# A graph network with experts on one Trainium2 core: edge stages in a fixed program order with work in small pieces, and VectorE's two-tensor operations reading both operands from SBUF

## The chip, the cores and the metric

The kernel runs on one core of a Trainium2 chip. The metric is the device time of one launch, in microseconds (us); lower is better. The time before is 2635.79 us, the median of three runs (2631.52 to 2639.92).

## The reference, cut to what matters

`x` has 3,125 nodes of 256 numbers. There are 53,125 edges (each node's edge to itself among them), each with a source, a destination, one of 200 types and a weight, all in float32 or int32. Four blocks follow one another, and each adds its result to `x`:

```python
ln = layernorm                                   # over the 256 numbers, no scale or offset
# 1: attention over neighbours, 4 heads of 64
feats = ln(x) @ Ws + bs                          # 4 heads
w = exp(-relu((a_s[src] + a_d[dst] + aw_e * edge_weight + ab) / 20))
x = x + segment_sum(w * feats[dst], src) / segment_sum(w, src)
# 2: 16 experts, each node through its best two
x = x + sum over top 2 of p_e * ((silu(ln(x) @ w1_e) * (ln(x) @ w2_e)) @ w3_e)
# 3: relations; h = ln(x)
W = W3 @ a                                       # three parts: source, destination, type
alpha = exp(leaky_relu(h[src] @ W_s + h[dst] @ W_d + rel[type] @ W_r))
alpha = alpha / sum(alpha, axis=1)               # over an axis of one element
agg = segment_sum((h[src] + rel[type]) @ weight_neighbor * alpha, dst)
x = x + relu(agg) + h @ (loop_weight where the node has an edge, else evolve_loop_weight)
# 4: FFN (256 to 1024 to 256, gelu) of the best half of the nodes by a score; h = ln(x)
s = h @ wr + br
x = x + (h + (gelu(h @ w1 + b1) @ w2 + b2) * s where the rank of s < 1561, else h)
```

## The kernel before, in words

**Tiles.** Nodes lie in 25 tiles of 128, one node per partition. Edges are sorted by the node that receives, so each node tile has its own stretch of edge tiles of 128 edges: 18 for a full tile, 8 for the last, 440 in all. Edge tiles are taken in groups of up to six (`GRP`), never across a node tile: 74 groups (`edge_groups`, L714).

**Stages in order** (`run`, L1477). Sort of the edges for the first layer (`sort_edges`, L310: a ranking that is a generator, whose `yield`s mark where other work may go between; then 13 moves, L545 to L569; then `load`, L578). Layer norm and features of the first layer, written to DRAM as `table0` (`heads_features`, L828). First edge stage, E0 (`heads_edges`, L881). Top two of 16 experts and the experts on 65 tiles of rows (`experts`, L989), and at the end of it 50 gathers `yg` (L1170) that fetch each node's two results, weighted and added to `x` by VectorE (L1174). Features of the second layer: products of its weights with `w3a` (L1203), tables of the types, layer norm `xn2`, and `table1` in DRAM (`relations_features`, L1181, with the store at L1270). Second edge stage, E1 (`relations_edges`, L1272, with `load` of the second sort ahead of it). Ranking of the nodes and FFN (`depths`, L1367).

**An edge stage** has three stages per group, which are functions that `edge_stages` (L724) returns. `gather`: for the first group of a node tile, SP fetches the node numbers of all its edges into every partition (`spread`, L739); GpSimd issues six indirect DMAs, one per edge tile, that bring one table row per edge into `rows` (L754, three buffers); VectorE makes `oh`, the one-hot of the receiving node per edge (L762, 128 x 768 numbers), and `hot` (L771), which has nodes or types on the partitions. `message`: TensorE multiplies `hot` with the receiving nodes' part of the score (L780), VectorE reduces it (L787), adds the parts of the score, and ScalarE takes exp. In E0 VectorE then multiplies the rows with the weights into `msg` (L926). In E1 it writes the one-hot of the type behind the row in `rows` (L1313, 200 numbers), and ScalarE scales `oh` into `ohw` (L1319). `add`: TensorE multiplies `oh` and `msg`, or `ohw` and `rows`, into the sums of the node tile (L798), and after its last group VectorE adds what lies beyond (`acc`) and calls `finish`. In E0 that divides by the sum of weights, adds to `x` and calls `done` of `gate` (L949), which for each five node tiles does the layer norm, stores it as `xtab` for the experts and computes the logits. In E1 it is L1324: loop weights and relations.

**What sets the order.** `pipelined` (L811) emits, for each step, one piece of the fill (in E0 the ranking of the second sort), then `gather` of group g, `message` of g-1 and `add` of g-2. This is the order in which the program is traced, not the order of issue: a list scheduler of the framework then orders each engine's instructions by its own estimates of when they are ready. [...]

**Operands in PSUM.** `edge_stages` takes a bank of PSUM, `hold`. It keeps `numbers` (0, 1, 2, ... along the free axis, a copy of an `iota`), which `oh` and the one-hot of the type compare with, and `weights_ps`, into which ScalarE writes the exp a second time for `msg` to read. So `oh`, `msg` and the type's one-hot each read one operand from PSUM and one from SBUF. One pool of PSUM serves the whole kernel: two tiles of 1024 numbers (`A`) and four of 512 (`B`).

**Ranking.** `depths` normalizes all nodes (`xn3`), takes the scores `wc`, turns them into a row `wrow` on every partition and, for each tile, counts the nodes that stand ahead of each of its nodes: `cmp` (L1426), over all 3,125, and `eq` (L1431) for ties. Only then does the FFN begin (L1445 on), four node tiles at a time.

Of the kernel before, what the change touches and what calls it, by code (L numbers as in the profile page):

```python
# [18 lines left out]
P = 128  # L19
# [3 lines left out]
class _Kernel:  # L23
# [12 lines left out]
    def __init__(self, ctx, tc, a, out):  # L36
# [18 lines left out]
        for b in range(self.NT):  # L55
# [7 lines left out]
        assert self.MT % self.KB == 0  # L63
# [3 lines left out]
        self.psum = ctx.enter_context(  # L67
            tc.tile_pool(name="psum", bufs=1, space=bass.MemoryType.PSUM)
        )
# [5 lines left out]

    def ps_a(self, name):
        return self.psum.tile([P, 1024], F32, tag="A", name=name, bufs=2)

    def ps_b(self, name):
        return self.psum.tile([P, 512], F32, tag="B", name=name, bufs=4)  # L80
# [17 lines left out]
    def constants(self):  # L98
# [14 lines left out]
        iota_i = self.work.tile([P, 512], I32, name="iota_i", bufs=1)  # L113
        nc.gpsimd.iota(iota_i, pattern=[[1, 512]], base=0, channel_multiplier=0)
        self.iota = c.tile([P, 512], F32, name="iota")
        nc.vector.tensor_copy(self.iota, iota_i)
# [51 lines left out]
    def transposed(self, src, n, name, evac=None):  # L168

        nc, c = self.nc, n // P  # L170
        pt = self.ps_b(f"ps_{name}")
        for i in range(c):
            nc.tensor.transpose(pt[:, i * P : (i + 1) * P], src[:, i * P : (i + 1) * P], self.ident)  # L173
        dst = self.work.tile([P, c, P], F32, tag=f"T{c}", name=name, bufs=3)
        (evac or nc.scalar.copy)(dst.rearrange("p c q -> p (c q)"), pt[:, :n])  # L175
        return dst
# [133 lines left out]
    def sort_edges(self, pool, rp, name, seg, other, value, bits, tab, help, roomy):  # L310
# [23 lines left out]
        def load_in():  # L334
# [6 lines left out]
            yield  # L341
# [23 lines left out]
            yield  # L365

        def places():
# [4 lines left out]
            for b0 in range(0, NT, piece):  # L372
                m = min(piece, NT - b0)
                hot = tl([P, piece, EC], BF16, "hot", bufs=1)
                for b in range(b0, b0 + m):
                    eng = nc.vector if b % 3 == 0 else help
                    eng.tensor_scalar(hot[:, b - b0, :], bf, float(b), None, op0=OP.is_equal)
                    if b % 6 == 5:
                        yield
                hv = hot.rearrange("p b (s t) -> p b s t", t=C)  # L380
                for w, ps in ((self.ones_h, tot), (self.before_h, pre)):
# [5 lines left out]
                    yield  # L387
# [39 lines left out]
            yield  # L427
# [3 lines left out]
            for b in range(NT):  # L431
# [13 lines left out]
                yield  # L445
# [39 lines left out]
            for s in range(NS):  # L485
# [13 lines left out]
                if s % 3 == 2:  # L499
                    yield  # L500
# [77 lines left out]
        def load():  # L578
# [4 lines left out]
            wide = [self.dram.tile([MT, P], BF16, name=f"{name}_w{i}") for i in range(1 + (not bits))]  # L583
            with tc.tile_pool(name=f"{name}_back", bufs=1) as bp:
# [13 lines left out]
                def turned(v):  # L598
                    pt = self.psum.tile([P, 1024], F16, tag="B", name=f"{name}_pt", bufs=4)
# [13 lines left out]
                for i, w in enumerate(wide):  # L613
                    wb = bp.tile([P, nb, P], BF16, name=f"{name}_wb{i}")
                    nc.vector.tensor_copy(wb[:m], tk[:m, :, :, 1 + i])
                    nc.sync.dma_start(w.rearrange("(i k) p -> k i p", k=m), wb[:m])
# [107 lines left out]
    def edge_stages(self, pool, st, table, width, into, near, others, messages, W, sums, finish):  # L724
# [4 lines left out]
        nc, G = self.nc, self.GRP  # L729
        nv = near.shape[3]  # L730
        now = {}


        hold, sums2 = self.ps_a("ps_hold"), self.ps_a("ps_sums")
        numbers = hold[:, :256]
        nc.vector.tensor_copy(numbers, self.iota[:, :256])
        self.numbers, self.weights_ps = numbers, hold[:, 512:]

        def spread(i, b):  # L739

            t = pool.tile([P, self.tiles[0] // 2, 2 * P + 8], BF16, name=f"wide{i}")
            src = st["wide"][i][self.first[b] : self.first[b] + self.tiles[b], :]
            src = src.rearrange("(o k i) p -> o k (i p)", o=1, i=2)
            nc.sync.dma_start(
                t[:, : self.tiles[b] // 2, : 2 * P], src.to_broadcast([P, self.tiles[b] // 2, 2 * P])
            )
            return t

        def gather(g, b, k, n, head, last):
            if head:  # L750
                now[b] = [spread(i, b) for i in range(len(st["wide"]))]
            rows = pool.tile([P, G, into], F32, name="rows", bufs=3)
            for j in range(n):
# [5 lines left out]
                )  # L759
            sh = [P, n, P]  # L760
            oh = pool.tile([P, G, P], F32, name="oh", bufs=3)
# [4 lines left out]
            lo = (k - self.first[b]) // 2  # L766
            hots = []
            for i, (at, _) in enumerate([(self.pcol1, None)] + others):
                w = now[b][min(i, 1)][:, lo : lo + n // 2, : 2 * P]
                t = pool.tile([P, G // 2, 2 * P], BF16, name=f"hot{i}", bufs=2)  # L770
                nc.vector.tensor_scalar(t[:, : n // 2, :], w, at, None, op0=OP.is_equal)  # L771
                hots.append(t)
            return rows, oh, hots

        def message(g, b, k, n, head, last, rows, oh, hots):
            pe = self.ps_b("ps_near")
            picks = [near[:, b]] + [v for _, v in others]
            for j in range(n):
                for i, (t, v) in enumerate(zip(hots, picks)):
# [6 lines left out]
            own = pool.tile([P, G, nv], F32, name="near")  # L786
# [4 lines left out]
            return messages(k, n, rows, own, oh)  # L791

        def add(g, b, k, n, head, last, oh, msg):
            if head:
                now["sum"] = sums2[:, b % 2 * 512 : (b % 2 + 1) * 512]
            ps = now["sum"]
            for j in range(n):
                nc.tensor.matmul(  # L798
                    ps[:, :W], oh[:, j, :], msg[:, j, :],
                    start=(head and j == 0), stop=(last and j == n - 1),  # L800
                )
            if last:
                more = pool.tile([P, W], F32, name="more")
                nc.sync.dma_start(more, sums[b])
                acc = pool.tile([P, W], F32, name="acc")
                nc.vector.tensor_add(acc, ps[:, :W], more)
                finish(b, acc)

        return gather, message, add

    def pipelined(self, stages, fill=()):  # L811


        groups, done = self.edge_groups(), {}
        fill = iter(fill)
        for step in range(len(groups) + len(stages) - 1):
            if step > 2:
                next(fill, None)
            for i, stage in enumerate(stages):
                g = step - i  # L820
                if 0 <= g < len(groups):
                    done[g] = stage(g, *groups[g], *(done.pop(g, None) or ()))
        for _ in fill:
            pass
# [56 lines left out]
    def heads_edges(self, st, fill, done):  # L881
# [26 lines left out]
        with self.tc.tile_pool(name="edge0", bufs=2) as pool:  # L908
# [7 lines left out]
            def messages(k, n, rows, near, oh):  # L916
# [6 lines left out]
                w = self.weights_ps[:, : n * H].rearrange("p (j h) -> p j h", h=H)  # L923
                nc.scalar.activation(w, s, AF.Exp)  # L924
                nc.scalar.activation(msg[:, :n, HO:], s, AF.Exp)
# [7 lines left out]
            def finish(b, acc):  # L933
# [7 lines left out]
                done(b)  # L941

            self.pipelined(self.edge_stages(
                pool, st, self.table0, W, W, near, [], messages, W, self.sums0, finish
            ), fill)
# [3 lines left out]
    def gate(self, pool):  # L949
# [16 lines left out]
        def done(b):  # L966
# [4 lines left out]
            self.norm_tiles(xn, t0, t1)  # L971
            nc.sync.dma_start(xv[:, t0:t1, :], xn[:, t0:t1, :])
            pl = self.ps_b("ps_logit")
            for t in range(t0, t1):
                xt = self.transposed(xn[:, t, :], D, "x_t")
                for c in range(C):
                    nc.tensor.matmul(
                        pl[:, (t - t0) * NE : (t - t0 + 1) * NE], xt[:, c, :], gw[:, c, :],
                        start=(c == 0), stop=(c == C - 1),
                    )  # L980
            nc.vector.tensor_tensor(
                self.logits[:, t0:t1, :],
# [575 lines left out]
```

## Time and profile before

| | us |
|---|---|
| median of three runs | 2635.79 |
| profiled execution, its own time | 2845.15 |
| its span in the trace | 2842.8 |
| TensorE busy / weight loads | 1878.6 / 1126.4 |
| VectorE busy | 1446.3 |
| ScalarE busy | 390.7 |
| GpSimd busy | 1167.4 |
| mean granted TensorE clock | 0.822 of full |

The profiled execution is 209 us longer than the median; durations below are from it. By operations in the timeline, the stages are: sort and first features up to 430 us, E0 to 1178, routing to 1217, experts to 1718, gather of the results to 1791, second features to 1870, E1 to 2563, ranking to 2682, FFN to the end.

How to read it: a row of operations gives line, engine, operation, output and inputs, number, then busy time and mean duration in ns, then the engine's idle time just ahead of them and what ended it ("issue" is time in which nothing that the profile shows was awaited). Engines are PE (TensorE), PEld (its weight loads), DVE (VectorE), ACT (ScalarE), POOL (GpSimd) and SP (which issues DMAs). In the table by stretch each engine has its busy time and its number of instructions, followed by the granted clock, the share of time that DMA engines were busy, and GB/s. The timeline has start, duration, engine, line and operation.

### The profile page before, as it was taken

The numbers are of one execution on the slowest core, as the hardware profiler recorded it, in microseconds if no ns is written. First come the engines' busy times: TensorE is split into PE (matmuls) and PEld (weight loads), VectorE is DVE, ScalarE is ACT, GpSimd is POOL, SyncE is SP. The second block draws the span as 40 slices with busy tenths as digits, with TensorE's granted clock in tenths as the row PEclk, the third lists the DMA queues.
The fourth block names the chain that finished last, engine by engine and source line by source line (L and its number), as shares of the span: only waits on it lengthen the run. The fifth ranks groups of instructions, "written<-read, shape, count | busy, mean of one in ns | idle before, by whom it ended". The sixth has DMA issues, their size and how long they took to land.

```text
span 2842.8 us, 24381 instructions
## 1 busy us (share of the span) xinstructions
PE 1878.6 (66%) x7534; PEld 1126.4 (40%) x7534; DVE 1446.3 (51%) x3397; ACT 390.7 (14%) x1097; POOL 1167.4 (41%) x1198
## 2 busy tenths in 40 slices
PE   3169554854544443399999991447878778785298
PEld 0024232543433332356666660323434334343166
DVE  4876225476665343644422224445655556549721
ACT  0000010010000000100112120112222222221012
POOL 4235306576654646034411115036666666650000
PEclk9999996676666667577799996768889888898599
DMA  2000325343444433144499982254545455431000
GB/s 83 0 3 5 104 89 137 93 130 112 115 100 114 116 100 101 49 150 130 131 316 318 317 291 84 87 156 131 148 129 148 130 142 149 128 85 34 8 21 18
DMA packets 258938, 334.04 MB, mean 118 GB/s; under 512 B 30861, under 2 KB 192407, under 8 KB 258807
## 3 DMA queue, kind: packets, MB, share of 16 engines
q1 hardware_dynamic: 197527, 191.26, 21.3%
q0 software_dynamic: 51920, 132.68, 17.6%
q10 hardware_dynamic: 9360, 8.52, 0.9%
q8 instruction: 61, 1.00, 0.1%
q14 instruction: 70, 0.57, 0.1%
HBM read 298.38 MB, written 33.98 MB: 117 GB/s over the span
## 4 chain that ended last, share of the span: by engine, by line
PE 39%; DVE 14%; issue 10%; POOL 9%; another core or an unknown queue 8%; DMA 4%; ACT 1%; SPq 0%; DVEq 0%; POOLq 0%; ACTq 0%
PE ps_sums L798 10%; PE ps_h L1130 9%; POOL rows L754 9%; PE ps_y L1147 4%; PE s_mv L560 3%; DVE cmp L1426 3%; PE ps_hid L1453 3%; PE ps_out L1464 3%; DMA rows<-table,s_idx 3%; DVE msg L926 2%; DVE hot L771 2%; PE ps_x_t L173 1%; PE ps_h_t L173 1%; PE ps_f L1264 1%
## 5 line engine op out<-in xcount | busy, mean ns | idle before, releaser
L754 POOL DMA_INDIRECT rows<-table,s_idx x880 | 848.6, 964 | 725.0 <-issue 240.4
L798 PE MATMUL ps_sums<-msg,oh 128*128 128x260 f32 x880 | 306.6, 519 | 261.8 <-DVE msg L926 143.1
L798 PE MATMUL ps_sums<-rows,ohw 128*128 128x457 f32 x880 | 414.0, 616 | 62.8 <-ACT ohw L1319 54.1
L798 PEld LDWEIGHTS ps_sums<-msg,oh 128*128 128x128 f32 x880 | 226.6, 265 | 325.1 <-issue 250.1
L560 PE MATMUL s_mv<-s_hv,s_hp 128*128 128x200 f16 (+1 forms) x832 | 246.8, 472 | 89.9 <-DVE s_hv L555 89.9
L798 PEld LDWEIGHTS ps_sums<-rows,ohw 128*128 128x128 f32 x880 | 179.0, 215 | 217.5 <-issue 149.6
L1130 PE MATMUL ps_h<-w,x_t 128*128 128x512 f32 x520 | 256.1, 638 | 0.0
L771 DVE TENSOR_SCALAR hot<-wide,pcols 128x768 bf16<-128x768 bf16 (+1 forms) x296 | 175.4, 597 | 73.9 <-PE ps_near L780 63.0
L560 PEld LDWEIGHTS <-s_hp 128*128 128x128 f16 x832 | 122.1, 147 | 208.7 <-issue 180.3
L762 DVE TENSOR_TENSOR oh<-ps_hold,s_row 128x768 f32<-128x768 f32 (+1 forms) x148 | 139.9, 946 | 125.7 <-remote 73.5
L1119 POOL DMA_INDIRECT xg<-xtab,who x65 | 61.9, 952 | 345.1 <-PE ps_x_t L173 302.6
L569 POOL DMA_INDIRECT s_tab<-s_rec,s_to x130 | 147.8, 1137 | 115.1 <-ACT s_rec L566 78.9
L780 PEld LDWEIGHTS <-hot 128*128 128x128 bf16 x1760 | 70.0, 98 | 212.3 <-issue 149.2
L1136 DVE TENSOR_TENSOR hid<-hid,ps_h 128x512 f32<-128x512 f32 x65 | 44.7, 688 | 210.3 <-ACT hid L1135 204.4
L1319 ACT ACTIVATE ohw<-oh,s 128x128 f32<-128x128 f32 x440 | 136.5, 388 | 106.6 <-DVE s L1282 75.2
L1130 PEld LDWEIGHTS ps_h<-w,x_t 128*128 128x128 f32 x520 | 102.8, 209 | 105.7 <-issue 105.5
L926 DVE TENSOR_TENSOR msg<-rows,ps_hold 128x1536 f32<-128x1536 f32 x74 | 128.1, 1731 | 2.0 <-ACT ps_hold L924 1.9
L787 DVE TENSOR_REDUCE near<-ps_near 128x24 f32<-128x72 f32 (+2 forms) x148 | 29.4, 198 | 190.3 <-remote 150.2
L1147 PE MATMUL ps_y<-w,h_t 128*128 128x256 f32 x520 | 122.9, 379 | 0.7 <-ACT h_t L175 0.7
L1147 PEld LDWEIGHTS ps_y<-w,h_t 128*128 128x128 f32 x520 | 98.7, 190 | 41.7 <-issue 30.6
L545 DVE TENSOR_TENSOR s_hp<-num_p,s_pp 128x1024 f16<-128x1024 f16 x104 | 71.8, 690 | 82.8 <-PE s_mv L560 81.4
L1313 DVE TENSOR_TENSOR rows<-ps_hold,s_val 128x1200 f32<-128x1200 f32 x74 | 101.1, 1367 | 6.1 <-PE ps_sums L798 6.1
(307 smaller groups left out, 2344.2 us busy)
## 6 DMA issues: line engine op xcount, KB each, us to landing
w<-in_L_ffn_w_dram SPq DMA_DIRECT2D x195, 512.0 KB
wide<-s_w SPq DMA_DIRECT2D x72, 576.0 KB
rows<-table,s_idx POOLq DMA_INDIRECT x880
ytab<-y ACTq DMA_DIRECT2D x65, 128.0 KB
sums<-sums_z SPq DMA_DIRECT2D x5, 1142.5 KB
more<-sums SPq DMA_DIRECT2D x25, 228.5 KB
sums<-sums_z SPq DMA_DIRECT2D x5, 650.0 KB
table<-f SPq DMA_DIRECT2D x5, 650.0 KB
```

The costliest lines, as they stand in the source:

```text
L560: nc.tensor.matmul(ps[:, : NK * V], hp[:, :, j], rec[:, :, :, j].rearrange("p k v -> p (k v)"), start=(j0 + j == 0), stop=(j0 + j == C - 1),)
L569: d = nc.gpsimd.indirect_dma_start(out=tab, out_offset=bass.IndirectOffsetOnAxis(ap=to[:, i : i + 1], axis=0), in_=out[:, k * CH * V : (k ...
L754: nc.gpsimd.indirect_dma_start(out=rows[:, j, :width], out_offset=None, in_=table, in_offset=bass.IndirectOffsetOnAxis(ap=st["idx"][:, k + ...
L762: nc.vector.tensor_tensor(oh[:, :n, :], numbers[:, None, :P].to_broadcast(sh), st["row"][:, k : k + n, None].to_broadcast(sh), op=OP.is_equal,
L771: nc.vector.tensor_scalar(t[:, : n // 2, :], w, at, None, op0=OP.is_equal)
L798: nc.tensor.matmul(ps[:, :W], oh[:, j, :], msg[:, j, :], start=(head and j == 0), stop=(last and j == n - 1),)
L926: nc.vector.tensor_tensor(msg[:, :n, :HO].rearrange("p j (h o) -> p j h o", o=O), rows[:, :n, :HO].rearrange("p j (h o) -> p j h o", o=O), ...
L1130: nc.tensor.matmul(ph[:, i * HID : (i + 1) * HID], xt[:, c, :], w12[:, i, c, :], start=(c == 0), stop=(c == C - 1),)
L1147: nc.tensor.matmul(py[:, :D], ht[:, c, :], w3[:, c, :], start=(c == 0), stop=(c == HC - 1))
L1313: nc.vector.tensor_tensor(rows[:, :n, R0:], self.numbers[:, None, :R].to_broadcast(sh), st["val"][:, k : k + n, None].to_broadcast(sh), op ...
L1319: nc.scalar.activation(ow[:, j, :], oh[:, j, :], AF.Copy, scale=s[:, 1, j : j + 1])
L1426: nc.vector.tensor_scalar(cmp[:, s:e], wrow[:, s:e], w, None, op0=op, op1=OP.add, accum_out=rank[:, t, i : i + 1],)
```

## The change

**Order.** `edges` takes the place of `edge_stages` and `pipelined`. Inside `tc.manual_schedule()` the instructions of each engine are issued in the order in which the program traces them, and the program writes that order out per step: node numbers of group g+2, gathers of g, a part of what closes a node tile, one-hots of g (and the type's in E1), messages and sums of g-1, another part, and pieces of other work up to a cost of 2.2. **Pieces.** That other work is a queue of generators that yield a cost: in E0 the ranking of the second sort (2.6 a piece) and `gate` (1.2 and 1.0), in E1 the new ranking of nodes. `finish` of both stages becomes a generator too.

```diff
+        def close(b):
+            acc = pool.tile([P, W], F32, name="acc")
+            nc.vector.tensor_add(acc, bank.pop(b)[:, :W], more.pop(b))
+            yield from finish(b, acc)
...
+        with tc.manual_schedule():
+            spread(0)
+            spread(1)
+            for g in range(len(groups) + 3):
+                if g + 2 < len(groups):
+                    spread(g + 2)
+                if g < len(groups):
+                    rows = gather(g)
+                if g >= 3 and groups[g - 3][4]:
+                    closers.append(close(groups[g - 3][0]))
+                go_on()
+                if g < len(groups):
+                    live[g] = rows, *hots(g)
+                    if prepare:
+                        prepare(*groups[g][1:3], rows)
+                if 0 <= g - 1 < len(groups):
+                    message(g - 1)
+                go_on()
+                piece(2.2)
+            while closers:
+                go_on()
+            piece(1e9)
```

`go_on` takes each closer one `yield` further; `piece(most)` takes pieces from the head of the queue until their costs reach `most`. In `hots`, `hot` now comes ahead of `oh`, and TensorE's products for the score follow at once. `message` also issues the products for the sums.

**Operands.** `hold` is gone. `numbers` is the `iota` in SBUF, and E0's weights are the columns of `msg` that ScalarE writes anyway, so that one exp goes:

```diff
-        numbers = hold[:, :256]
-        nc.vector.tensor_copy(numbers, self.iota[:, :256])
-        self.numbers, self.weights_ps = numbers, hold[:, 512:]
+        numbers = self.iota[:, :256]
...
-                w = self.weights_ps[:, : n * H].rearrange("p (j h) -> p j h", h=H)
+                w = msg[:, :n, HO:]
                 nc.scalar.activation(w, s, AF.Exp)
-                nc.scalar.activation(msg[:, :n, HO:], s, AF.Exp)
...
+            def prepare(k, n, rows):
+                sh = [P, n, R]
+                nc.vector.tensor_tensor(
+                    rows[:, :n, R0:], self.iota[:, None, :R].to_broadcast(sh),
+                    st["val"][:, k : k + n, None].to_broadcast(sh), op=OP.is_equal,
+                )
```

(`prepare` held the same lines inside `messages` before, with `self.numbers`.)

**Buffers.** PSUM is taken anew for each part of the kernel: `A` 2 and `B` 4 as before, but in the edge stages `near` 2, `sums` 2 and `B` 4, of one bank each. `rows` has 3 buffers in E0 and 4 in E1, `oh` 3 and 2. The node numbers are fetched group by group (three buffers each) instead of per node tile, from rows in DRAM that hold a padding of 8, so that each is one contiguous piece; they are written by two DMAs instead of one.

**Second features.** `relations_features` becomes a generator. Its part on weights stands ahead of the experts; its layer norm, products and stores go, for each four node tiles, behind the addition of the experts' results of that tile. `load` of the second sort now follows in the same block of buffers.

```diff
                         self.x[:, t, :], yg, top[i][:, t : t + 1], self.x[:, t, :],
                         op0=OP.mult, op1=OP.add,
                     )
+                done(t)
...
-                    self.experts([lambda f=f: f(moves) for f in steps])
-        self.relations_features()
-        self.relations_edges(load())
-        self.depths()
+                with self.banks(**general):
+                    features = self.relations_features()
+                    with tc.tile_pool(name="move1", bufs=1) as moves:
+                        self.experts([lambda f=f: f(moves) for f in steps], next(features))
+                        next(features, None)
+                    st = load()
+        with tc.tile_pool(name="route", bufs=1) as pool:
+            with self.banks(**at_edges):
+                self.router(pool)
+                self.rows_bufs, self.oh_bufs = 4, 2
+                self.relations_edges(st)
+            with self.banks(**general):
+                self.depths()
```

**Ranking beside E1.** `router` loads the weights of the FFN and of the score ahead of E1. `finish` of E1 queues `route(t)`; at tiles 5, 10, 15, 20, 23 and 25 it normalizes the tiles since the last time, takes their scores, extends the row and counts: for the old tiles the new columns only, for the new tiles all columns so far.

```diff
+            end = min(N, t1 * P)
+            for t in range(t0):
+                count(t, t0 * P, end, OP.is_gt, 3 + i)
+                if t % 3 == 2:
+                    yield 2.2
+            for t in range(t0, t1):
+                lo, hi = t * P, min(N, (t + 1) * P)
+                count(t, 0, lo, OP.is_ge, 0)
+                count(t, lo, end, OP.is_gt, 1)
```

`depths` keeps the sum of the counts and the FFN.

## The prediction

> **What bounds the kernel now.** I first read the busy time of each engine by stage (stretches cut where the operations of one stage begin and end).
>
> ```profile
> core 0: us, PE busy (x) PEld busy (x) DVE busy (x) ACT busy (x) POOL busy (x), PEclk, DMA share, GB/s
> 430.00:1178.00 748.00, 387.43 (x1598) 285.17 (x1598) 413.58 (x980) 53.87 (x194) 433.61 (x442) 0.68 0.40 108
> 1178.00:1217.00 39.00, 8.02 (x55) 7.32 (x56) 30.23 (x95) 5.22 (x18) 2.86 (x3) 0.50 0.37 128
> 1718.00:1791.00 73.00, 0.00 (x0) 0.00 (x0) 35.27 (x103) 0.56 (x2) 47.58 (x50) 0.52 0.31 90
> 1791.00:1870.00 79.00, 41.37 (x186) 29.46 (x186) 31.62 (x95) 9.30 (x25) 0.00 (x0) 0.82 0.27 90
> 1870.00:2563.00 693.00, 530.36 (x2499) 268.14 (x2500) 382.34 (x966) 174.15 (x591) 415.96 (x440) 0.86 0.50 135
> 2563.00:2682.00 119.00, 35.38 (x137) 24.73 (x136) 115.28 (x237) 11.62 (x19) 0.29 (x1) 0.66 0.06 20
> 2682.00:2843.00 161.00, 152.81 (x567) 102.73 (x565) 31.52 (x72) 36.32 (x60) 0.00 (x0) 0.98 0.06 20
> ```
>
> These are the first edge stage (E0), routing, the gather of the experts' results, the second layer's features, the second edge stage (E1), the ranking of nodes (VectorE alone: 115 of 119 us) and the last FFN. Sorting before 430 and the experts (1217 to 1718) are left out. No engine is full in E0; TensorE is busiest in E1. Next, GpSimd's gathers in E0 and in E1:
>
> ```profile
> L754 POOL DMA_INDIRECT rows<-table,s_idx x440 | 432.7, 983 | 381.5 <-DVE msg L926 161.5 <-issue 123.1 <-DVE near0p L651 85.7
> L754 POOL DMA_INDIRECT rows<-table,s_idx x440 | 416.0, 945 | 343.5 <-issue 117.3 <-DVE near1p L651 85.4 <-PE ps_sums L798 73.8
> ```
>
> The 85 us are the wait for the stage to begin. A gather takes 0.945 us and another follows 0.30 us later ("issue"), so a group of six needs 6 x 1.245 = 7.5 us at least, while E0's 440 gathers run from 430 to 1158 (728 us, 9.8 per group of 74) and E1's from 1871 to 2545 (674, 9.1). The rest is waiting: 161 us in E0 for `msg`, which frees `rows`, and 138 us in E1 (gaps over 0.35 us summed along the timeline) for TensorE. Last, the timeline, for who disturbs a gather:
>
> ```profile
> 711.83 1.02 DVE L437 TENSOR_TENSOR_SCAN s_cum<-at_block,s_x 128x416 f32<-128x416 f32 x1
> 712.07 1.54 POOL L754 DMA_INDIRECT rows<-table,s_idx  x1 [0.31 <-issue]
> 712.77 1.73 DVE L926 TENSOR_TENSOR msg<-rows,ps_hold 128x1536 f32<-128x1536 f32 x1
> 713.91 0.95 POOL L754 DMA_INDIRECT rows<-table,s_idx  x1 [0.30 <-issue]
> ```
>
> The scan reads two SBUF tensors; the gather under it ends 0.76 us after the scan does and takes 1.54. The next one, beside `msg` (one operand in PSUM), takes 0.95. Over all gathers that meet an operation 0.2 us after their start: 97 met `oh` and 69 met `msg`, both with no mean extension; 17 met the scan (+0.43 us), 29 met `s_hv`, two SBUF tensors as well (+0.51).
>
> [...] So `oh` shouldn't get shorter from SBUF; the trace agrees: `s_pos` (SBUF twice) takes 0.586 us for 416 elements, `oh` 0.952 for 768, the same line of some 1.04 ns an element plus 0.15.
>
> **The change part by part** (in the profiled execution: span 2842.8, 2845.15 with what lies around it; the median of the runs shown is 2635.79, so I carry the saving over as a share).
>
> *Edge stages, fixed order.* Per step GpSimd is issued gather g, while VectorE makes the one-hots of g and the messages of g-1. Rows have 3 buffers in E0 and 4 in E1, and what frees them is two or more groups old when GpSimd comes to them. So the waits for `msg` and TensorE should go, and next is GpSimd itself: 7.5 us per group plus the port. [...] An operation of T us then holds it up T²/2.5 on average where T is under 1.25, and T - 0.625 where it is longer. E0: `msg` (1.745) costs 1.12, `oh` (0.952) 0.36, the sort's own operations as now (983 - 945 ns, x 6 = 0.23): 7.5 + 1.7 = 9.2, x 74 = 681 us in place of 728: -47. E1: `oh` and the relation one-hot (1.378) stand back to back; [...] so I take 0.77 rather than 0.36 + 0.75, and 0.25 for the ranking's operations: 8.5, x 74 = 629 in place of 674: -45. No cost (bound from below): 7.8 and 7.7. Every operation costing its full length: 10.2 and 9.9.
>
> Can the others keep up? VectorE in E0: 413.6/74 = 5.6 us, and 0.45 for waiting on ScalarE's exp, which now stands in its stream with the scores behind it: 6.1 of 9.2. That slack also covers the landing of a gather (3 to 5 us in the chain of waits), behind which VectorE's fill pieces now stand. In E1: (382.3 - 14.5 for norms)/74 = 5.0, plus 0.45, plus ranking work 1.7 (below): 7.1 of 8.5, single groups 9. TensorE in E1: 530/74 = 7.2. All below GpSimd, E1 only just; without that cover E1 gains nothing.
>
> *Other edits there, at nothing.* One exp fewer (ScalarE is 7% busy in E0); the wide rows in 74 and 148 small SP transfers in place of 25 and 50 (0.37 us of issue each, two groups ahead[...]); PSUM banks renamed by stage. E1's closing passes through steps with ranking pieces between: +6 us. `w1` and `w2` (2 MB) go ahead of its first transfers on SP, about 7 us of DMA at the experts' 300 GB/s; the fourth rows buffer covers it.
>
> *Features of layer 2.* Weight work (1799.7 to 1811) moves ahead of routing: six products of 0.88, six copies of 0.4 and some twenty small operations, 12 us on VectorE's critical stretch; nothing is counted as hidden: +12 (0 to 20, since the 2.4 MB of `w3a` might be awaited). Norms, transposes and tables move beside the gather of results: VectorE gets 25 x (0.33 + 0.38) = 18 us on top of 35 of 73, so I add 5. After the last x: one norm 2, three tiles at 1.87 (their period from 1811 on) 5.6, then table store to first gather 12 as now (1858.5 to 1870.9): 19. 73 + 79 = 152 becomes 78 + 19 = 97: -55 (-75 to -35).
>
> *Ranking beside E1.* From last x (2563.7) to the FFN's first matmul it is 119 us. In the new order VectorE still has after the last x: one tile's counts 3.4; norm and scores of three tiles 8.3; 20 counts of 384 columns at 0.6, 12; three tiles at 3.79 (the period of a tile from 2642 on), 11.4; norm and scores of two tiles 4. Only then is the row transposed that TensorE awaits ahead of the FFN: 39. The last 23 short counts and two tiles (17 us) lie beside the FFN's first 16 us: -80. All ranking work is 115 + 14.5 + 73 added counts x 0.3 = 152; less some 58 at the end, 94 over about 55 groups is the 1.7 above.
>
> Sum: -47 + 12 - 55 - 45 + 6 - 80 = -209. 209/2845 is 7.3%, and 2635.8 less 7.3% is 2442: 2440.
>
> **The rivals.** *The port costs little* (gathers slip between VectorE's operations): E0 577 (-151), E1 570 (-104); sum -372, 2291. For it: the 43 gathers that met the sort's `s_hp` (line 545, two SBUF tensors as well) were held up by 0.12 us in the mean; against it: the scan and `s_hv`. *The port costs every operation in full*: E0 755 (+27), E1 733 (+59); sum -31, 2607: the moved tails alone pay. For it: GpSimd's s_tab transfers average 1.137 us beside such operations. *Slower: VectorE's stream in fixed order becomes the bound*, in both edge stages. If at each step it waits out the landing of a gather (5 us) on top of 6 us of work, a group takes 11 us: E0 814 (+86), E1 814 (+140 and 6); the other parts give -123; sum +109, 2737. It decides from 0.8 us a group above today's (10.6 and 9.9). Against it: GpSimd may run two groups ahead.
>
> **How the numbers follow.** Likeliest 0.55 (2440), little port cost 0.17, full port cost 0.18, slower 0.10. Range 2290 to 2610 reaches the ends of the two port cases and leaves out the slower one and little else. 0.3%, 8 us, is about what a measurement of this kernel can tell from no change; the full port case lies 1% below and may lose a part of its saving: same 0.03, faster 0.87, slower 0.10.
>
> **What would show it.** Right: gathers in E0 mostly at 1.0 to 1.3 us mean (983 now), hardly any of GpSimd's idle over 0.35 us, extensions only under `oh`, `msg` and the relation one-hot; E0's gathers span about 680 us, E1's 630; some 40 us between last x and FFN; the first E1 gather about 90 to 100 us after the first gather of results. Wrong: gathers at 0.95 with gaps still (VectorE or TensorE binds), or a mean over 1.4.

## The result, and the profile after

The changed kernel takes 2776.64 us (median of four runs, 2773.21 to 2780.47) against 2635.78 before: a ratio of 1.0535 (95% interval 1.0512 to 1.0558). It is slower by 141 us, where 2440 was predicted.

The profile shown with the prediction was of an execution of 2845 us that took 209 us longer than the median (no other run of the kernel before, here or below, took over 2653); a second trace of that kernel (span 2639.1 us, `before_again` below) is the one to compare with. The busy times of the engines by stage, the kernel before first; the stretches are E0's gathers, the gather of results with the second features, E1's gathers, and everything after the last addition to `x`.

```profile
core 0: us, PE busy (x) PEld busy (x) DVE busy (x) ACT busy (x) POOL busy (x), PEclk, DMA share, GB/s
430.00:1016.00 586.00, 361.69 (x1558) 268.18 (x1558) 403.88 (x952) 49.85 (x185) 433.50 (x440) 0.73 0.50 137
1574.00:1721.00 147.00, 42.62 (x186) 30.38 (x186) 67.03 (x198) 9.63 (x26) 47.26 (x50) 0.68 0.30 93
1721.00:2342.00 621.00, 496.79 (x2453) 259.62 (x2454) 377.34 (x943) 168.25 (x574) 416.21 (x440) 0.89 0.55 150
2361.00:2639.00 278.00, 187.68 (x700) 127.55 (x700) 145.41 (x306) 48.00 (x79) 0.07 (x1) 0.84 0.06 20
```

And the same stretches of the changed kernel:

```profile
430.00:1091.00 661.00, 401.79 (x1549) 297.26 (x1550) 449.30 (x965) 39.77 (x110) 481.99 (x440) 0.70 0.46 123
1669.00:1774.00 105.00, 54.16 (x163) 35.39 (x163) 53.72 (x173) 11.07 (x32) 48.34 (x52) 0.60 0.38 117
1774.00:2511.00 737.00, 520.92 (x2425) 272.42 (x2426) 461.20 (x1121) 176.25 (x584) 499.79 (x440) 0.84 0.46 128
2548.00:2777.00 229.00, 183.13 (x679) 123.24 (x679) 85.50 (x229) 45.62 (x75) 0.00 (x0) 0.91 0.04 14
```

Both edge stages got longer: E0 by 75 us, E1 by 116. GpSimd's busy time in them rose by 48 and 84 us for the same 440 gathers. The two tails that the change moves did get shorter, by 42 and 50 us. Cut at the same events in both timelines (first and last gather of each edge stage, last `acc` addition, first expert product, first `yg`, last addition to `x`), the 138 us between the two spans fall as follows:

| stretch | before, us | after, us | difference | predicted |
|---|---|---|---|---|
| E0's gathers | 585.6 | 660.5 | +75 | -47 |
| to the first expert product | 59.1 | 79.1 | +20 | +12 |
| experts | 499.2 | 498.9 | 0 | 0 |
| gather of results, features | 147.2 | 105.2 | -42 | -55 |
| E1's gathers | 621.1 | 736.6 | +116 | -45 |
| to the last addition to `x` | 18.2 | 37.8 | +20 | +6 |
| ranking (what is left) and FFN, to the end of the span | 278.5 | 228.5 | -50 | -80 |

What GpSimd waited for in E1: the gathers' row of the kernel before, then of the changed one.

```profile
L754 POOL DMA_INDIRECT rows<-table,s_idx x440 | 416.6, 947 | 289.6 <-issue 119.1 <-DVE near1p L651 85.0 <-PE ps_sums L798 68.3
```

```profile
L811 POOL DMA_INDIRECT rows<-table,s_idx x440 | 499.8, 1136 | 247.5 <-issue 115.2 <-PE ps_sums L859 94.8 <-DVE near1p L692 10.7
```

The same two rows for E0:

```profile
L754 POOL DMA_INDIRECT rows<-table,s_idx x440 | 433.5, 985 | 238.7 <-issue 120.3 <-DVE near0p L651 86.6 <-DVE msg L926 18.4
L811 POOL DMA_INDIRECT rows<-table,s_idx x440 | 482.0, 1095 | 264.1 <-issue 123.1 <-DVE near0p L690 85.6 <-DVE msg L996 47.8
```

In E1, two things at once: a gather takes 1.136 us instead of 0.947, and in spite of a fourth buffer of rows GpSimd waits 95 us for TensorE to release one. VectorE's waits in the same stretch say why (columns: engine, operation waited with, its releaser, us in total, times, longest).

```profile
DVE agg L1441 <- PE ps_rel L1428: 120.6, 22, 6.3
DVE s L1366 <- ACT s L1365: 75.5, 71, 4.6
DVE ln_rs L192 <- ACT ln_rs L190: 29.6, 4, 7.4
```

In the second trace of the kernel before, `agg` waits 10.2 us in all for `ps_rel`. The timeline of the changed kernel shows both costs within 15 us:

```profile
2094.37 0.42 ACT L1422 COPY ct<-ps_cnt 128x128 f32<-128x128 f32 x2 [5.04 <-PE ps_cnt L1418]
...
2095.21 0.19 DVE L1366 RECIPROCAL s<-s 128x6 f32<-128x6 f32 x1 [3.07 <-ACT s L1365]
...
2096.09 4.88 PE L859 MATMUL ps_sums<-rows,ohw 128*128 128x457 f32 x12 [1.10 <-ACT ohw L1406]
...
2100.80 1.03 PE L1428 MATMUL ps_rel<-rel_w,ct 128*128 128x257 f32 x4
...
2101.87 0.42 DVE L1441 TENSOR_TENSOR agg<-acc,ps_rel 128x256 f32<-128x256 f32 x1 [6.27 <-PE ps_rel L1428]
...
2104.51 1.64 DVE L825 TENSOR_SCALAR hot<-wide,pcols 128x768 bf16<-128x768 bf16 x3
...
2106.07 0.95 DVE L831 TENSOR_TENSOR oh<-iota,s_row 128x768 f32<-128x768 f32 x1
...
2106.52 2.63 POOL L811 DMA_INDIRECT rows<-table,s_idx  x1 [0.30 <-DVE hot L825]
...
2106.93 1.40 DVE L1395 TENSOR_TENSOR rows<-iota,s_val 128x1200 f32<-128x1200 f32 x1
...
2109.46 0.95 POOL L811 DMA_INDIRECT rows<-table,s_idx  x1 [0.30 <-issue]
```

`ps_rel` stands behind the sums of the next group on TensorE, these wait for `ohw`, and `agg` stands at the head of VectorE's stream: the one-hots of the group after that, which need neither, are held up by 6.27 us. ScalarE's stream has the same trouble on a smaller scale: its copies `ct` for the tile that closes wait 5.04 us for TensorE, the exp of the next group stands behind them, and so VectorE waits 3.07 us for `s`. Then `oh` and the type's one-hot run without a break, and the gather that began under `oh` takes 2.63 us instead of 0.95: it ends 0.82 us after the second has ended.

### The profile page after: what moved, and what is told of

The parts are those of the page before. It is cut to its first block, busy times and chain, and to the rows that moved or that the text cites. A ratio compares the mean times of both kernels' runs of the same rounds, so it can differ in the third digit from the quotient of the medians.

```text
span 2777.0 us, 24660 instructions
## 1 busy us (share of the span) xinstructions
PE 1938.6 (70%) x7534; PEld 1173.5 (42%) x7534; DVE 1534.3 (55%) x3581; ACT 391.4 (14%) x1045; POOL 1301.2 (47%) x1198
## 5 line engine op out<-in xcount | busy, mean ns | idle before, releaser
L811 POOL DMA_INDIRECT rows<-table,s_idx x880 | 981.8, 1116 | 511.6 <-issue 238.2
L859 PE MATMUL ps_sums<-rows,ohw 128*128 128x457 f32 x880 | 425.1, 639 | 138.1 <-ACT ohw L1406 137.3
L859 PE MATMUL ps_sums<-msg,oh 128*128 128x260 f32 x880 | 347.8, 573 | 230.2 <-DVE msg L996 230.2
L859 PEld LDWEIGHTS ps_sums<-msg,oh 128*128 128x128 f32 x880 | 251.0, 294 | 295.1 <-DVE msg L996 236.4
L859 PEld LDWEIGHTS ps_sums<-rows,ohw 128*128 128x128 f32 x880 | 189.2, 223 | 325.8 <-ACT ohw L1406 171.0
L825 DVE TENSOR_SCALAR hot<-wide,pcols 128x768 bf16<-128x768 bf16 (+1 forms) x296 | 164.9, 598 | 5.3 <-DMA wide<-s_w 5.3
L996 DVE TENSOR_TENSOR msg<-rows,msg 128x1536 f32<-128x1536 f32 x74 | 129.2, 1745 | 32.1 <-ACT msg L995 32.1
L831 DVE TENSOR_TENSOR oh<-iota,s_row 128x768 f32<-128x768 f32 (+1 forms) x148 | 139.3, 941 | 4.8 <-ACT ohw L1406 4.8
L1501 DVE TENSOR_SCALAR_CACHE_REDUCE cmp<-wrow,wc 128x640 bf16<-128x640 f32 (+16 forms) x122 | 107.2, 878 | 5.9 <-ACT wrow L1529 2.8
L1395 DVE TENSOR_TENSOR rows<-iota,s_val 128x1200 f32<-128x1200 f32 x74 | 102.9, 1390 | 0.0
## 6 DMA issues: line engine op xcount, KB each, us to landing
more<-sums SPq DMA_DIRECT2D x25, 228.5 KB
```

What stands on the lines that cost most here:

```text
L811: nc.gpsimd.indirect_dma_start(out=rows[:, j, :width], out_offset=None, in_=table, in_offset=bass.IndirectOffsetOnAxis(ap=st["idx"][:, k + ...
L825: nc.vector.tensor_scalar(t[:, : n // 2, :], wide[g][min(i, 1)], at, None, op0=OP.is_equal)
L831: nc.vector.tensor_tensor(oh[:, :n, :], numbers[:, None, :P].to_broadcast(sh), st["row"][:, k : k + n, None].to_broadcast(sh), op=OP.is_equal,
L859: nc.tensor.matmul(bank[b][:, :W], oh[:, j, :], msg[:, j, :], start=(head and j == 0), stop=(last and j == n - 1),)
L996: nc.vector.tensor_tensor(msg[:, :n, :HO].rearrange("p j (h o) -> p j h o", o=O), rows[:, :n, :HO].rearrange("p j (h o) -> p j h o", o=O), ...
L1395: nc.vector.tensor_tensor(rows[:, :n, R0:], self.iota[:, None, :R].to_broadcast(sh), st["val"][:, k : k + n, None].to_broadcast(sh), op=OP ...
```

## The experiments

Two theories. **Order:** the stream that is written out puts VectorE in front of results that TensorE delivers late, and what stands behind has nothing to do with them. **Port:** VectorE's operations with two SBUF inputs hold up GpSimd's gathers. "Port" is a name here, in the prediction and in the expectations: measured is that a gather beside such operations ended later (in E1 1.136 us in the mean for 0.947); what in the chip makes it wait was not shown. Rivals to both are named with the runs. E0 and E1 stand below for the time from the first to the end of the last gather of the stage, each from one trace: an E0 that no edit touched took 660 to 666 us in four traces of the changed kernel and its variants, so differences of some 6 us say nothing. Each ratio is to the kernel before beside that run, whose medians were 2642 to 2645 us there, 6 to 9 above the 2636 beside the result; differences to 2777 us are uncertain by as much.

**`before_again`: the kernel before, unchanged.**

> The kernel before, unchanged. Its profiled execution took 2845 us where its other runs took 2636, and the 209 us are missing from the prediction's account. In the trace, VectorE waits some 310 us for a release of unknown origin ahead of near, oh and acc, mostly once per node tile. Theory 'waiting for node numbers': these are waits for the transfers of the node numbers (512-byte pieces), which are long in that one execution only; then a new profiled execution shows either 2636 us with few such waits, or 2840 us with them all. Rival, 'another cause': a new trace of about 2840 us without these waits, or of 2636 us with them.

It took 2642.34 us (ratio 0.9994, interval 0.9981 to 1.0006), its profiled execution spans 2639.1. These are VectorE's waits in the trace that the prediction read (`remote`: the profile doesn't show what ended them):

```profile
DVE near L787 <- remote: 150.2, 30, 12.3
...
DVE oh L762 <- remote: 73.5, 9, 14.0
DVE acc L806 <- remote: 70.8, 6, 18.4
```

In the new trace no wait has an unknown origin; what it has is this, in E0:

```profile
DVE s L919 <- DMA rows<-table,s_idx: 107.6, 32, 9.4
DVE near L787 <- PE ps_near L780: 33.2, 8, 7.6
```

E0's gathers take 586 us there instead of 728, E1's 621 instead of 674. So the 295 us of waits of unknown origin belong to that one execution; what caused them stays open. What the prediction took for the edge stages' loss was mostly not there in an ordinary run.

**`after_psum`: the changed kernel with the operands of before.**

```diff
-        numbers = self.iota[:, :256]
+        hold = self.ps("hold", "ps_hold")
+        numbers = hold[:, :256]
+        nc.vector.tensor_copy(numbers, self.iota[:, :256])
+        self.numbers, self.weights_ps = numbers, hold[:, 256:]
...
-        at_edges = dict(near=2, sums=2, B=4)
+        at_edges = dict(near=2, sums=2, hold=1, B=3)
```

> The changed kernel with the operands of before: numbers for oh and the type's one-hot, and E0's weights, in a bank of PSUM of their own (the second exp comes back, the general PSUM tiles of the edge stages go from 4 to 3). Port theory: what makes the change slow is that VectorE's operations with two SBUF operands hold up GpSimd's gathers; a gather goes from 1.10 and 1.14 us to 0.95 to 1.0, E0 from 660 to about 600 us, E1 from 737 to about 640, the whole from 2777 to about 2620. Order theory: the fixed order itself makes E1 slow, VectorE's stream standing at agg and at ln_rs for TensorE and ScalarE; gathers get shorter, but E1 stays over 700 us and the whole over 2720.

2754.19 us (ratio 1.0416, 1.0391 to 1.0442). E0 fell from 660 to 630, E1 only from 737 to 731: the gathers were back at 0.948 us, and the time turned into waiting.

```profile
L814 POOL DMA_INDIRECT rows<-table,s_idx x440 | 417.3, 948 | 324.3 <-PE ps_sums L862 143.5 <-issue 118.2 <-DVE hot L828 16.3
```

The wait for TensorE rose from 95 to 144 us. So the longer gathers (1.136 us in the changed kernel) don't set E1's pace as long as VectorE stands at `agg` (120.6 us there). In E0 they cost 30 us. The order theory holds for E1, the port theory for part of E0.

**`before_sbuf`: the kernel before with operands in SBUF alone.**

```diff
-        numbers = hold[:, :256]
-        nc.vector.tensor_copy(numbers, self.iota[:, :256])
+        numbers = self.iota[:, :256]
...
-                w = self.weights_ps[:, : n * H].rearrange("p (j h) -> p j h", h=H)
+                w = msg[:, :n, HO:]
                 nc.scalar.activation(w, s, AF.Exp)
-                nc.scalar.activation(msg[:, :n, HO:], s, AF.Exp)
```

> The kernel before with nothing changed but the operands: numbers is the iota in SBUF, E0's weights are read from msg in SBUF, one exp goes. Port theory: gathers lengthen to 1.1 us in the mean, and the time goes up by 80 to 160 us to 2715 to 2795. Order theory: the scheduled order has room for that, under 2670 us.

2709.68 us (ratio 1.0245, 1.0221 to 1.0270): +65, between the two. E0 went from 586 to 671 (a gather 1.203 us instead of 0.985), and E1, unforeseen by both, from 621 to 604, although its gathers rose from 0.947 to 1.045.

**`before_wide`: the kernel before with contiguous node numbers.**

```diff
...
-            src = src.rearrange("(o k i) p -> o k (i p)", o=1, i=2)
+            src = src.rearrange("(o k) r -> o (k r)", o=1)
...
```

> The kernel before with the node numbers as the changed kernel stores them: rows of 264 numbers with a padding of 8, so that each node tile's numbers are one contiguous piece of 4752 bytes per partition, written by two transfers; still one transfer per node tile. Theory 'waiting for node numbers': the profiled execution no longer takes 209 us more than the others, the unknown waits shrink to under 60 us, and the timed runs stay at 2636 within 1%. Rival: the profiled execution stays near 2840 us.

2640.05 us (ratio 0.9979, 0.9969 to 0.9990), profiled span 2640.6, no unknown waits. As `before_again` has none either, the run says nothing on what the unknown waits were; it does say that making these transfers contiguous is worth 0.1 to 0.3%.

**`agg_late`: `agg` one `yield`, half a step, later.**

```diff
                         start=(c == 0), stop=(c == C - 1),
                     )
                 yield
+                yield
                 xt = self.x[:, t, :]
                 v = pool.tile([P, D], F32, name="agg")
```

> The changed kernel with one more yield in E1's finish between TensorE's products for relations and loops and VectorE's agg, so that agg stands behind the one-hots and the messages of the next group instead of ahead of them. Order theory: agg's 121 us of waiting (22 times 5.5, TensorE being still at the sums issued ahead of ps_rel) hold up the next group's one-hots and with them the sums and the rows; the wait falls under 30 us, E1 goes from 737 to 640 to 680, the whole from 2777 to 2680 to 2720. Ranking theory: it is the ranking's 90 us of VectorE work that E1 can't take; the wait moves to other operations, and E1 stays over 715.

2695.03 us (ratio 1.0201, 1.0180 to 1.0221): one line takes back 82 of the 141 us (88 by the ratios). E1 falls to 645.

```profile
DVE agg L1442 <- PE ps_rel L1428: 14.2, 14, 2.2
```

```profile
L811 POOL DMA_INDIRECT rows<-table,s_idx x440 | 497.2, 1130 | 159.0 <-issue 113.0 <-PE ps_sums L859 15.4 <-DVE near1p L692 10.7
```

The wait went from 120.6 to 14.2 us, and GpSimd's for TensorE from 95 to 15: what is left is mostly its own pace, with gathers of 1.130 us where `after_psum` has 0.948. The order theory's numbers are met; the ranking theory's (over 715) are not.

**`rank_after` and `agg_late_rank_after`: ranking worked off after E1, alone and with `agg` late.**

```diff
-                self.queue.append(self.route(t))
+                self.later.append(self.route(t))
...
             while closers:
                 go_on()
+            self.queue.extend(self.later)
             piece(1e9)
```

> The changed kernel with the ranking of nodes kept in a list and worked off after E1, in the same pieces. Ranking theory: E1 goes from 737 to about 650, and as much comes back behind the last x, some 229 + 90; the whole stays near 2777 or falls by up to 30. Order theory: agg's waiting (121 us) stays, E1 gives back 30 to 50 (the wait for ln_rs and some of VectorE's work), the tail grows by 90, the whole goes to 2820 to 2840.

> Both edits at once: E1 with the fixed order, neither agg's wait nor ranking. If these two are what makes E1 slower than in the kernel before with SBUF operands (604 us), E1 comes to 600 to 625 and the whole to about 2740 (the tail 90 us longer). If something else in the fixed order costs, E1 stays over 650.

2826.28 us (ratio 1.0699, 1.0674 to 1.0724) and 2764.52 (1.0457, 1.0430 to 1.0484). Alone, E1 gets 72 us shorter (665), more than the order theory said, although `agg` waits as before:

```profile
DVE agg L1442 <- PE ps_rel L1429: 139.6, 22, 8.0
```

The end from the last addition to `x` gets 109 longer (338 for 228): the whole is 50 us worse, as only that theory had it. With `agg` late, E1 comes to 619 and the whole to 70 us more than `agg_late` (some 25 more than expected). So the ranking beside E1 costs E1 27 us once the wait is gone (645 against 619), some 20 more on the way to the last addition, and saves 110. With the wait there it costs 72: VectorE's work and its waits stand in one stream, and in E1 of the changed kernel they fill it, 461 us of work and 265 of waits in 737. Taking away either part relieves it, and the two gains, 91 and 72, are 118 together.

**`logits_late`: one addition of the logits per block of tiles, a step later.**

```diff
...
-                    nc.vector.tensor_add(self.logits[:, t - 1, :], pl[:, :NE], self.gate_b)
-                if t < t1:
-                    yield 1.0
+                yield 1.0
+            yield 2.2
+            nc.vector.tensor_tensor(
+                self.logits[:, t0:t1, :],
+                pl[:, : (t1 - t0) * NE].rearrange("p (t e) -> p t e", e=NE),
+                self.gate_b[:, None, :].to_broadcast([P, t1 - t0, NE]), op=OP.add,
+            )
```

> The changed kernel with the gate's additions of the logits, one per block of tiles, a step behind its products (in the changed kernel each tile's addition stands right behind its product: 20 waits of 2.9 us, TensorE being at sums). Order theory: the 59 us of waiting fall under 15, E0 goes from 660 to 615 to 640, the whole to 2730 to 2755. Port theory: [...] E0 stays over 650 and the whole over 2765.

(The change had also split the addition per block, as the kernel before has it, into one per tile; the edit undoes that too, and no run separates fewer additions from later ones.) 2762.25 us (ratio 1.0459, 1.0437 to 1.0481): -14 (-20 by the ratios), a little less than expected in the whole; E0 fell as expected, by 22 us to 639. The wait in question in the changed kernel,

```profile
DVE logits L1056 <- PE ps_logit L1053: 58.6, 20, 6.8
```

has no row left in the new trace. Of the 59 us E0 gets 22 back: two other waits of VectorE rose in their place, for rows to land from 53 to 69 us and of `msg` for the exp from 32 to 48. The port theory's bound (over 650) is not met.

**`fixed_late_psum` and `fixed_late_psum0`: both additions late, operands in PSUM in both edge stages, or in E0 alone.** The edits are those of `agg_late`, `logits_late` and `after_psum` together; in the second, `numbers` is the iota again in E1, and E1 has its fourth `B` bank.

> The changed kernel with agg a step later (as in agg_late), the logits' additions per block a step later (as in logits_late) and the operands in PSUM (as in after_psum). If the waits in VectorE's fixed stream and the port are the two costs, E0 goes from 660 to 600 to 615 (-22 and -30 were seen one by one), and E1, which with agg late has nothing left but GpSimd (gathers of 1.13 us, 15 us of gaps), from 645 to 590 to 620: the whole to about 2590. Rival, 'VectorE's stream binds E1 anyway': as in after_psum the shorter gathers turn into gaps, E1 stays at 635 to 650, the whole at 2635.

> The same with the operands in PSUM in E0 only and in SBUF in E1. Port theory: E1 at 645 as in agg_late, E0 at 600 to 615, the whole about 2640, some 40 us above the version with PSUM in both. Rival: no difference from the version with PSUM in both in E1 (within 10 us).

2599.20 us (ratio 0.9822, 0.9796 to 0.9849) and 2622.18 (0.9927, 0.9899 to 0.9955). Both beat the kernel before. E0 takes 598 and 592, E1 616 with PSUM and 642 without: with the waits gone, operands in SBUF cost 26 us in E1 after all, where they cost 6 (737 against 731) while `agg` set the pace. The medians lie 23 us apart, less than the 40 expected; the four runs of the second spread over 24 us, and its trace is of the fastest, so its stages are rather too short.

**`before_features` and `before_features_sbuf1`: the kernel before with the second features beside the gather of results; then also with `numbers` in SBUF in E1.**

```diff
-        self.relations_features()
-        self.relations_edges(load())
+        self.relations_edges(st)
...
-        numbers = hold[:, :256]
-        nc.vector.tensor_copy(numbers, self.iota[:, :256])
+        if into == self.W0:
+            numbers = hold[:, :256]
+            nc.vector.tensor_copy(numbers, self.iota[:, :256])
+        else:
+            numbers = self.iota[:, :256]
```

(The lines ahead of "..." are in both, those behind it in the second only.)

> The kernel before with one part of the change: the second features as a generator, its weights' part ahead of the experts and its norms, products and stores beside the gather of the results. If the part is worth what the profiles of the two kernels show, the time from the first gather of results to E1's first row goes from 147 to about 105 us, routing gets some 11 longer, and the whole goes from 2640 to 2605 to 2615. Rival: the scheduler, which orders by its own estimate, places them late again, and the time stays within 8 us of 2640.

> The same, and in E1 alone VectorE's one-hots read both operands from SBUF (in before_sbuf E1 went from 621 to 604 us while E0 lost 85). If that gain belongs to E1's operands, the whole is some 17 us under the version with the features alone: 2588 to 2598. If it came from elsewhere (the different order that the scheduler makes), within 8 us of it.

2613.70 us (ratio 0.9879, 0.9846 to 0.9912) and 2588.51 (0.9790, 0.9762 to 0.9819), the fastest version here. The gather of results and the features take 99 and 96 us (147 before), routing 11 more, E1 629 and 604. The second gain is not shown to be the operands': the scheduler, given one dependence less, also puts the type's one-hot elsewhere in VectorE's stream, and no run separates the two.

## Why the prediction was wrong, by its steps

*What bounds the kernel now* failed first. "E0's 440 gathers run from 430 to 1158 ... and E1's from 1871 to 2545 ... The rest is waiting" was true of the execution shown and of no other trace. The 209 us by which it exceeds the median were noted and then spread over the kernel as a share. With the second trace as base, the same steps give 681 - 586 = +95 for E0, 629 - 621 = +8 for E1, 97 - 147 = -50 for the features, and with +12, +6 and -80 a sum of -9: 2630, no real gain. That is 190 of the 337 us between 2440 and 2777.

*Edge stages, fixed order.* That E0 came out at 8.93 us a group where 9.2 were predicted is luck. The longer gathers cost 0.9 us a group there (1.095 us for 0.945), half of the 1.7 that was put in for the port; waits for `msg` (47.8 us, 0.65 a group), which "should go", made up for most of the rest. That an operation of T us holds up a gather by T²/2.5 or T - 0.625 was the author's estimate; of what the prediction shows, the gather under the scan speaks for it (1.54 us for 0.95). `msg` cost 0.55 and not 1.12, since gathers didn't meet it at random: beside 38 of the 72 `msg` of that stretch, a gather began 1.1 to 1.3 us after `msg`, with at most 0.65 of its 1.745 us to go. In E1 the port was sized well: longer gathers cost 1.1 us a group in `agg_late` for 1.0, and 8.72 us in all for 8.5. That two operations back to back let a gather in between them, from which the 0.77 came, was an estimate too and mostly wrong: of the 51 gathers of E1 that began under `oh` in the changed kernel, 41 ended only 0.82 us after the type's one-hot and took 2.19 to 2.89 us.

*"Can the others keep up?"* is the step that failed in E1: 7.1 of 8.5 us. VectorE's work was put at 6.7 us a group and came to 6.2. The waits in its stream were put at 0.45 us, for the exp alone, and came to 3.6 (265 us): 121 us for `agg`, 76 for the exp, 30 for the square root of the ranking's norm. So work and waits make 9.8 us a group, more than GpSimd's pace. The largest term, what VectorE's stream waits for on TensorE when a node tile is closed, was left out; "E1's closing passes through steps with ranking pieces between: +6 us" looked at the pieces only. The runs put in its place 22 waits of 5.5 us; moving `agg` out of their way gave back 91 us of E1. The timeline shows both halves of it: on TensorE `ps_rel` begins at 2100.80, directly behind the sums (4.88 us from 2096.09); on VectorE `agg` begins at 2101.87 after 6.27 us of waiting, and `hot` and `oh` of the next group only behind it, at 2104.51 and 2106.07. In E0 the same happened at `logits`, 22 us.

E0's +75 taken apart: fixed order without those waits and with operands in PSUM +12 (598) or +6 (592); operands in SBUF +41 to +47 (639); the logits +22 (660). E1's +116: -6 (616) for the order with late `agg` and PSUM, +30 (645) for SBUF, +91 for `agg`. This is one order of taking the parts; with the ranking out first it is 72 for the ranking and 46 for `agg`, as above.

*Features* were right in kind: -42 instead of -55, 5 us of that because the stretch took 147 us and not 152 before. *Routing*: +11 of the +20 are the weights' part, as said; the rest is the last waits at `logits`, of 6 us each, which `logits_late` takes away (the last `acc` addition ends 12 us after E0's last gather there, 19 in the changed kernel and 11 before). *Ranking*: the time to the FFN's first product was 41 us (39 predicted), but the gain is 50 and not 80. "From last x (2563.7) to the FFN's first matmul it is 119 us" was misread: in that trace, as in the second one, the FFN's first product comes some 25 us after the last addition. TensorE's first 28 us of the FFN, 14.0 for `ps_hid` and 14.0 for `ps_out`, lay beside the ranking in the kernel before; here is the row of `ps_hid` alone in that stretch and in the rest:

```profile
core 0: us, PE busy (x) PEld busy (x) ACT busy (x), PEclk, DMA share, GB/s
2361.00:2478.00 117.00, 14.00 (x32) 6.00 (x32) 5.50 (x8) 0.66 0.07 20
2478.00:2639.00 161.00, 75.87 (x192) 34.43 (x192) 30.43 (x48) 0.98 0.06 20
```

Of the rivals, the slower one had the right end and place, VectorE's fixed stream, but the wrong wait: waiting for rows to land came to 53 us in E0 and 9 in E1, where it put 5 us on every group. Its 11 us a group came to 8.9 and 10.0; that its 2737 is near is owed to the same wrong base, from which the losses look smaller.

## What to carry to other kernels

Where an order is written out by hand, go through each engine's stream and ask of every instruction that reads another engine's result what stands ahead of that result on the other engine; if it is work of the next step, put the reader behind what doesn't need it (here 22 waits of 5.5 us at `agg` and 20 of 2.9 at `logits`). What an engine has to fit into a step is its work and the waits in its stream together (6.2 and 3.6 us a group for VectorE in E1). Before losses are read off a profile, see that its own time is that of the other runs; if it isn't, take the difference away first, or leave the stages that hold it out of the sum. What an operand moved between PSUM and SBUF was worth here went by what its engine's neighbours waited for: with the late additions, where GpSimd nearly sets the pace, it cost 41 to 47 us in E0 and 26 to 30 in E1; where VectorE stood at `agg` it cost 6, which is no more than two traces of the same code differ by.

## What the runs showed of the hardware

In E0 of the changed kernel, where `oh` and `msg` read SBUF twice, the three gathers that began 0.01 to 0.02 us after `msg` took their usual 0.95 us. The 120 that began later under one of the two, from 0.10 us on, all ended 0.81 to 0.83 us after that operation: 58 under `oh`, with 1.15 us in the mean, and 62 under `msg`, with 1.60. In the kernel before, with one operand in PSUM, those beside `oh` and `msg` were not extended in the mean (97 and 69 in the prediction's count). If a second such operation follows at once, the gather mostly ends behind that one, but not always: of the 51 that began under `oh` in E1 of the changed kernel, 41 ended 0.82 us after the type's one-hot (2.63 us for the one shown), and 10 ended 0.82 us after `oh`, half a us before the type's one-hot did. What decides isn't shown.
